# A four-layer graph network on one core: a new written order with layer 1 half a period later, the setup in thirteen steps, and layer 1's head outputs turned by DMA and VectorE

## The chip, the cores and the metric

The kernel runs on one core of a Trainium2 chip. The core has a matrix engine (TensorE, PE in the profile), a vector engine (VectorE, DVE), a scalar engine for activations (ScalarE, ACT), GpSimd (POOL) and a queue engine for transfers (SyncE, SP). Each works through its own instructions in order; semaphores tie them together. The metric is the device time in microseconds from the start of the program to its end; lower is better.

## The reference

Sixty-four graphs of 256 nodes with 256 features pass through four layers. Every layer adds its result to its input and normalizes the rows. `adj` (0 or 1) masks the attention in all of them.

```python
# layer 0: attention with 4 heads of 64, output projection, layer norm
q, k, v = (split(x @ W.T + b) for W, b in ((Wq, bq), (Wk, bk), (Wv, bv)))
attn = softmax(where(adj == 0, -1e9, q @ k.T * 64 ** -0.5))
x = norm(x + layer_norm((attn @ v) @ Wo.T + bo, gamma, beta))
# layer 1: attention with 8 heads of 32 of the normed rows with themselves, then an MLP
n = layer_norm(x, gamma1, beta1)
x2 = x + softmax(where(adj > 0, n @ n.T * 32 ** -0.5, -inf)) @ n      # by head
x = norm(x + x2 + gelu(layer_norm(x2, gamma2, beta2) @ W1 + b1) @ W2 + b2)
# layer 2: additive attention: leaky_relu(s1 + s2), masked softmax, times x @ W
# layer 3: leaky_relu((x * a0) @ x.T) where adj == 1, masked softmax, times x
```

All data are 32-bit floats.

## The kernel before

The 64 graphs make 32 groups of two. A group's work is cut into eleven generators ("threads"), each of which runs one step at a time: `a` (load, mask, layer 0's projections, scores, products of both graphs), and for each graph (0, 1) `u` (layer 0's output projection and norms), `z` (layer 1's input turned), `w` (layer 1's head outputs, norm, its result turned), `o` (the MLP's second product, layers 2 and 3, the store); `b` is layer 1's attention and `c` the MLP's first product with GELU, for both graphs.

What stands after what is written out. `PLACES` gives each step of a group a time in periods, a period being one group; `FIRST` and `LAST` spell the order of the filling and of the emptying pipeline, a letter for a thread and a digit for a group. A wrapper ties each engine's instructions in the order in which the steps issue them, SP's transfers included, so nothing overtakes: an instruction that waits holds up everything behind it on its engine. `BUFS` says how many buffers a tile has; a new tile waits until the oldest one's readers are done.

TensorE wants the contracted axis on partitions, so tiles are turned often. `flipped` does it in one of two ways: by `transpose` on TensorE into PSUM, which ACT copies out, or by `put` (two transfers to DRAM), `get` (four transfers back that place 32x32 blocks) and one block transpose on DVE (`turn_blocks`). The switches `FX`, `FZ`, `FY`, `FN2`, `FN3` choose the second way for x, layer 1's input (z), the MLP's input (xb) and the rows of layers 2 and 3 (xn); `DIRECT` lists exceptions by group. For layer 1's head outputs (oT in `thread_w`), `FO` is False: eight transposes a group on TensorE.

Layer 0's softmax sums go to DRAM and come back to all partitions (`lines`, then `rr`), in `thread_u`, before the head outputs are scaled.

Weights for the first steps are loaded by ACT's queue at the start. All others are gathered in the list `later`, and the generator `prepare` issues them on SP and works out what is derived from them (`bop`, the output bias with the values' bias; W1 times gamma2 and b1; the columns of `wx`; bounds), one of its seven steps after each of the turns in `PREPARE`.

ACT holds one table of functions at a time; between an exponential and a GELU a table load stands in its program.

Of the kernel before, what the change touches and what calls it, by code (L numbers as in the profile page):

```python
# [8 lines left out]
F32 = mybir.dt.float32  # L9
# [4 lines left out]
ALU = mybir.AluOpType  # L14
AX = mybir.AxisListType

P = 128
N = 256
D = 256
NC = D // P  # L20
# [4 lines left out]
W = D + 4  # L25
DFF = 1024
NF = DFF // P
# [12 lines left out]
FO = False  # L40
# [3 lines left out]
DIRECT = {0: ('x', 'z'), 31: ('yT', 'n2', 'n3')}  # L44
BUFS = {'t': 6, 'q': 3, 'k': 2, 'v': 5, 'y': 4, 'z': 4, 'xb': 4, 'both': 2, 'xn': 6, 'mask': 3, 'e': 6, 'x0': 2, 'turned': 1, 'blk': 3, 'oT': 2, 'zs': 2, 'rr': 2, 'xT': 1, 'qT': 1, 'kT': 1}
PLACES = {
    "a": (0.00000, 0.26380, 0.44172, 0.77301, 0.77914, 0.78528, 0.80982, 0.85890, 0.87730, 0.95092, 0.96932,
        0.99386, 1.04295, 1.07362, 1.08589, 1.11043, 1.12883, 1.13497, 1.17178, 1.18405, 1.19018, 1.21472,
        1.25767, 1.27607, 1.28221, 1.29448, 1.31902,),
    "u0": (1.33742, 1.34356, 1.34969, 1.40491, 1.41104, 1.49080, 1.54601, 1.56442, 1.60736, 1.68098,),  # L50
    "u1": (1.36810, 1.41718, 1.51534, 1.55215, 1.57055, 1.60123, 1.63190, 1.65031, 1.67485, 1.79141,),
    "z0": (1.61350, 1.66258, 1.69325, 1.72393,),
    "z1": (1.75460, 1.80368, 1.82209, 1.85276,),
    "b": (1.74847, 1.76074, 1.76687, 1.81595, 1.84049, 1.84663, 1.89571, 1.90184, 1.90797, 1.91411, 1.92024,
        1.92638, 1.93865, 1.95705, 1.96319, 1.98773,),
    "w0": (1.93251, 1.94478, 2.01841, 2.02454, 2.06135, 2.14110, 2.22086, 2.30675,),
    "w1": (2.01227, 2.03068, 2.03681, 2.09203, 2.14724, 2.20245, 2.23313, 2.31288,),
    "c": (2.32515, 2.38037, 2.48466, 2.50920, 2.53374, 2.57669, 2.58896, 2.61963,),
    "o0": (2.63804, 2.65644, 2.69939, 2.73620, 2.82822, 2.86503, 2.88957, 3.04908, 3.19632, 3.20859, 3.30061,
        3.33129, 3.37423, 3.38650, 3.39264, 3.42331, 3.43558, 3.46626, 3.47853, 3.52147, 3.58282, 3.62577,  # L60
        3.64417, 3.66871, 3.71779, 3.98159, 4.05521, 4.07975, 4.09816, 4.10429, 4.11656, 4.12270, 4.25153,
        4.59509,),
    "o1": (2.79755, 2.83436, 2.87117, 2.88344, 2.97546, 3.00614, 3.06749, 3.23926, 3.26994, 3.28834, 3.35583,
        3.36196, 3.42945, 3.44785, 3.45399, 3.46012, 3.47239, 3.49693, 3.50307, 3.55828, 3.68712, 3.70552,
        3.71166, 3.73006, 3.74233, 4.15337, 4.15951, 4.16564, 4.17791, 4.22699, 4.24540, 4.52761, 4.53988,
        5.39877,),
}
PREPARE = (8, 14, 26, 50, 70, 85, 100)
FIRST = (
    "a0a0a0a0a0a0a1a1a1a0a0a0a0a0a0a0a0a1a1a0a0a2a0a0a0a0a0a0a0a0a1a0a0a0U0U0U0a1a1U0a1u0u0a2U0U0u0u0U0U0U0Z0Z0u0"  # L70
    "u0u0u0a2Z0Z0U0b0b0b0b0u0z0b0a2z0z0b0z0b0b0b0b0b0b0W0W0a1b0b0b0a1b0a1W0W0W0W0w0u0w0w0w0W0a1a1a1a1a1a1a1a1a1a1"
    "W0a1w0a1a1a1w0w0w0c0a1c0U1U1c0c0U1U1u1U1U1u1u1c0a2a2c0c0c0u1O0O0U1U1U1Z1a2u1Z1u1U1u1u1O0u1o0O0Z1z1z1Z1b1b1b1"
    "O0z1o0o0o0u1z1b1b1b1a2a2b1b1b1b1b1b1O0O0W1W1b1o0a2b1b1a3a3a2a2b1o0O0a2w1W1W1W1o0o0w1w1w1a2a2a3a2a2a2a2a2W1W1"
    "a2a2w1w1w1O0O0a2a2a2W1o0a4o0U2U2w1a2a2u2u2o0o0c1c1O0O0o0o0o0o0o0c1u2c1o0o0o0U2O0O0O0O0U2c1O0O0O0U2U2c1U2U2O0"
    "O0c1c1u2U2Z2O1o0o0o0O1Z2u2u2O0O0o0a3o1U2O0u2u2o0Z2Z2u2O0O1O1z2a3a3b2b2b2o1o1o1a4z2z2b2b2b2z2a3a3a3b2b2b2b2b2"
    "b2b2b2a4a4O0O0W2O1O1W2O1a3a3b2b2o1o0o0a3a3o1W2W2w2W2W2u2w2w2O1w2O0O0a3a3a3a3o1a3W2W2O0O0w2w2w2a3a3a3a3O1o0o0"
    "o1o0o0O1a3a3a3U3U3o1o1a3w2O1a3c2O1U3o1c2o1O1O1O0O0U3U3U3u3u3u3o0o0o1o1o1o1c2c2O1U3U3c2c2O1O1u3U3Z3o1c2u3u3O1"
    "u3u3c2O1O2O2Z3o1u3Z3Z3O1O1u3b3o1o1O1O2O2z3o1O1O1o2O1O0b3b3b3o1o1z3b3O2z3O2O2o1o1b3o2o2a4z3b3a4b3a4O2b3b3b3b3"
    "b3o2a4a4O1O1b3O1O1a4a4W3b3a4U3W3W3W3o2b3w3o2o2O1a4a4a4a4w3w3a5W3O1w3")
LAST = (  # L80
    "a7w5a6o4o3o3O4O3a6a6a6W5W5o4a6o4o4U6U6w5a6u6u6c5c5o4O4U6o4o4o4O4o2o4o4U6U6U6o4o3c5c5c5O4o3O3c5a7o4o4U6U6U6Z6"
    "u6O4O4O4O4O4u6u6u6o4o4c5u6Z6u6c5O5Z6U6Z6b6O4O4o4O4u6z6z6O5b6b6b6u6O5O5O4z6b6o5b6O5O4O4O4o5a7o4o4a7a7z6b6o5o5"
    "b6a7b6b6b6b6W6W6b6a7a7b6a7a7W6W6O5O5b6b6o4o4o5o5o5a7w6w6w6O5a7a7a7a7O4w6a7a7O4O4O4W6W6a7a7a7w6w6o4O5o4o5O4O5"
    "a7a7O4a7a7W6o5o4o4W6w6w6o5o4a7U7o5U7a7U7o5u7u7c6c6U7O5o4o5O4O4U7O5c6u7c6U7o5o5U7U7U7Z7o5u7u7o3O5u7o5o5Z7O5O5"
    "O5u7u7Z7c6o5c6U7c6O5c6u7z7o5o5O6O6O6O5O6z7z7Z7b7b7o6b7b7u7o5O6O5O5O5b7b7O6O5o6o6o6z7b7O6b7b7O4b7b7W7b7O6W7o6"
    "o6o6b7b7o5o5O5O5O5b7b7w7O6W7O6o6w7o5o6o5o5o5w7W7o6O5W7o5o5w7O5w7o4O5o5W7W7O5O5O5O5w7w7O6w7W7c7c7O6O6o6O6O6o6"
    "c7c7o5O6O6c7O5O5o6o6o6o5o6c7c7c7o6o6O7O6O7O7O6O6o7o6O6O6O6O6O7O7o6o6o7o6O6o7O7O7o6o6O6O6o7o7O6O6O7O7o7O6o6O7"
    "O7O6o7o7O6o7o5o7o7O7o7O7O7O6O6O7O7O7o7o7o6o7o7o7o6o6o6o6o6O7o6O7O7O7o7o7O7o7o7o7O7O7O7o7o7o7O7O7O7o6O7O7o7o7"
    "O7o7O7O7o7o7o7o7O7o7o6o7")
LETTERS = dict(a="a", U="u0", u="u1", Z="z0", z="z1", b="b", W="w0", w="w1", c="c", O="o0", o="o1")  # L90
# [358 lines left out]
def usual_input(ctx: ExitStack, tc: tile.TileContext, a: dict, out: bass.AP, flag: bass.AP):  # L449
# [84 lines left out]
    def load(queue, to, of):  # L534
        if queue:
            queue.dma_start(to, of)
        else:
            later.append((to, of))

    def load_rows(name, cols, queue=None):  # L540

        src = a[name]
        t = const.tile([P, src.shape[0] // P, cols], F32, name=name)
        load(queue, t, src.rearrange("(c p) f -> p c f", p=P))
        return t
# [22 lines left out]
    beta0 = load_all(a["L0_gnn_beta"], "beta0", queue=ACT)  # L568
    woT = load_rows("L0_gnn_WoT", D)
    bv = load_column(a["L0_gnn_bv"], D, "bv")  # L570
    bo = load_all(a["L0_gnn_bo"], "bo", 0)

# [4 lines left out]
    gamma0 = load_all(a["L0_gnn_gamma"], "gamma0")  # L577
    beta1r = load_all(a["L1_gnn_beta1"], "beta1r")
    gamma1r = load_all(a["L1_gnn_gamma1"], "gamma1r", 256)
    b2 = load_all(a["L1_gnn_b2"], "b2", 512)  # L580
    gamma1 = load_column(a["L1_gnn_gamma1"], D, "gamma1")
    beta1 = load_column(a["L1_gnn_beta1"], D, "beta1")
    gamma2 = load_column(a["L1_gnn_gamma2"], D, "gamma2")
    beta2 = load_column(a["L1_gnn_beta2"], D, "beta2")
    b1 = load_column(a["L1_gnn_b1"], DFF, "b1")
    a0 = load_column(a["L3_gnn_a0"], D, "a0")
    w1 = load_rows("L1_gnn_W1", DFF)
    w2 = load_rows("L1_gnn_W2", D)
# [500 lines left out]

    def prepare():  # L1090

        for to, of in later[:3]:
            SP.dma_start(to, of)
        yield
        for to, of in later[3:-2]:
            SP.dma_start(to, of)
        yield
# [8 lines left out]
        for to, of in later[-2:]:  # L1106
            SP.dma_start(to, of)
        wa = setup[:, 1280:2304].rearrange("p (s c d) -> p s c d", s=2, c=NC)
        for s in range(2):
            DVE.tensor_tensor(wa[:, s], wx[:, :, 0:D], a12[:, s:s + 1, :].to_broadcast([P, NC, D]), ALU.mult)  # L1110
        DVE.tensor_reduce(wa1, wa, AX.X, ALU.add)
        for k, (s, share) in enumerate(((0, SLOPE - 1.0), (1, SLOPE), (1, 1.0))):
            DVE.tensor_scalar(wx[:, :, D + k:D + k + 1], wa1[:, s, :].unsqueeze(2), share, None, ALU.mult)

        yield
# [15 lines left out]

        yield
# [23 lines left out]
        yield  # L1156

        pm = new(ps_m, [P, NF], F32, "pm", 4)
        for f in range(NF):
            for c in range(NC):  # L1160
                matmul(pm[:, f:f + 1], w1[:, c, f * P:(f + 1) * P], beta2[:, c:c + 1], start=c == 0, stop=c == NC - 1)
        DVE.tensor_tensor(b1, b1, pm, ALU.add)
        for c in range(NC):
            DVE.tensor_scalar(w1[:, c, :], w1[:, c, :], gamma2[:, c:c + 1], None, ALU.mult)
# [7 lines left out]

    def written(text, since):
        return [(since + int(text[k + 1]), LETTERS[text[k]]) for k in range(0, len(text), 2)]

    preparing = prepare()
    groups = [threads_of(g) for g in range(B // G)]
    plan = [(g, n) for _, g, n in sorted((g + t, g, n) for g in range(B // G) for n, ts in PLACES.items() for t in ts)]
    head, tail = written(FIRST, 0), written(LAST, B // G - 8)
    for turn, (g, name) in enumerate(head + plan[len(head):len(plan) - len(tail)] + tail):  # L1180
        next(groups[g][name], END)
        if turn in PREPARE:
            next(preparing, END)
    assert next(preparing, END) == END
# [54 lines left out]
```

## Time and profile before

| what | us |
|---|---|
| median of 3 runs (2472.14 to 2473.8) | 2473.54 |
| time of the profiled execution | 2474.4 |
| span of the profiled execution, first to last instruction | 2472.5 |
| TensorE busy | 2414.1 (98%) |
| VectorE busy | 2119.0 (86%) |
| ScalarE busy | 1510.2 (61%) |
| GpSimd busy | 747.2 (30%) |

In a page's first part "busy" is time in which at least one instruction of that engine ran; the second part cuts the span into 40 slices, with busy tenths as digits. A row of a group names line, engine, operation, output and input tiles with shapes, how often it came, its busy time, the mean of one in ns, and the idle time ahead of it with what ended it. All recorded operations bear one line number, that of the wrapper, so rows are told apart by tiles. A row of the timeline gives start, length, engine, operation and how many.

### The profile page before, as it was taken

What the parts mean: (1) busy time and instruction counts of PE and PEld (TensorE: products, weight loads), DVE (VectorE), ACT (ScalarE), POOL (GpSimd) and SP (SyncE); (2) the same over time, 40 slices, a digit from 0 to 9 for tenths busy, and PEclk for the clock granted to TensorE, in tenths of its full rate; (3) what the DMA queues carried; (4) which work ended last, traced back from release to release, by engine and by line L of the source; (5) the groups of instructions that cost most, each with busy time, mean ns of one, the idle gap of its engine ahead of it and who ended that gap; (6) DMA issues with size and microseconds to landing.
All of it is one profiled execution on the core that took longest, in us unless ns stands there. A gap on an engine that the chain in (4) does not pass through costs nothing.

```text
span 2472.5 us, 48109 instructions
## 1 busy us (share of the span) xinstructions
PE 2414.1 (98%) x15888; PEld 1811.9 (73%) x15888; DVE 2119.0 (86%) x6238; ACT 1510.2 (61%) x2635; POOL 747.2 (30%) x1804
## 2 busy tenths in 40 slices
PE   5899999999999999999999999999999999999997
PEld 3577777777777777787777777777777777777776
DVE  4788888988888988889988889988888988889884
ACT  3456566666666666666666666665666666666654
POOL 0222233323233233233232333232333232333232
PEclk9899999999999999999999999999999999999999
DMA  6235253444443444443444444444444444434321
GB/s 143 46 82 108 61 112 88 92 98 101 96 103 86 92 97 101 101 103 86 91 96 102 103 96 91 89 99 103 103 87 96 92 99 101 106 85 92 81 65 44
DMA packets 903791, 229.78 MB, mean 93 GB/s; under 512 B 707313, under 2 KB 903153, under 8 KB 903537
## 3 DMA queue, kind: packets, MB, share of 16 engines
q1 hardware_dynamic: 902032, 225.73, 41.8%
q8 instruction: 128, 2.10, 0.4%
q14 instruction: 127, 1.03, 0.1%
q10 hardware_dynamic: 1504, 0.92, 0.1%
HBM read 136.07 MB, written 82.05 MB: 88 GB/s over the span
## 4 chain that ended last, share of the span: by engine, by line
PE 72%; ACT 8%; DVE 6%; DMA 5%; SPq 4%; POOL 3%; issue 2%; ACTq 0%; DVEq 0%; POOLq 0%
PE pm L473 65%; PE ps L473 7%; SPq L473 4%; DMA blk<-rows 3%; ACT e L473 2%; ACT adj L473 1%; DVE y L473 1%; DVE e L473 1%; ACT adjb L473 1%; POOL rstd L473 1%; ACT xn L473 1%; DVE st L473 1%; ACT xb L473 1%; POOL nm L473 1%; ACT oT L473 1%
## 5 line engine op out<-in xcount | busy, mean ns | idle before, releaser
L473 POOL TENSOR_SCALAR ve<-mv 128x2 f32<-128x2 f32 x448 | 149.3, 333 | 1613.9 <-DVE mv L473 1104.9
L473 PE MATMUL pm<-L_gnn_W,hT 128*128 128x256 f32 x2048 | 468.0, 382 | 0.0
L473 PE MATMUL pm<-t,L_gnn_W 128*128 128x256 f32 x2048 | 458.2, 379 | 1.6 <-DVE t L473 1.6
L473 ACT ACTIVATE e<-ps 128x1024 f32<-128x1024 f32 x384 | 373.0, 1021 | 126.1 <-PE ps L473 125.4
L473 PEld LDWEIGHTS pm<-L_gnn_W,hT 128*128 128x128 f32 x2048 | 382.0, 190 | 67.0 <-issue 18.9
L473 PEld LDWEIGHTS pm<-t,L_gnn_W 128*128 128x128 f32 x2048 | 386.5, 190 | 53.9 <-DVE t L473 2.1
L473 DVE SCALAR_TENSOR_TENSOR e<-e,mask 128x256 f32<-128x256 f32 x1024 | 364.7, 420 | 12.7 <-ACT e L473 12.4
L473 POOL TENSOR_TENSOR rstd<-ve,mhalf 128x2 f32<-128x2 f32 (+1 forms) x384 | 344.9, 898 | 32.0
L473 ACT ACTIVATE xn<-y,nm,rstd 128x256 f32<-128x256 f32 x256 | 139.5, 593 | 278.0 <-POOL xn L473 223.0
L473 DVE BATCH_NORM_STATS2 st<-y 128x6 f32<-128x256 f32 x640 | 236.3, 411 | 4.7
L473 DVE STREAM_TRANSPOSE t<-blk 128x512 f32<-128x512 f32 x248 | 172.1, 703 | 75.1 <-DMA blk<-rows 74.9
L473 ACT ACTIVATE hT<-pm,b 128x512 f32<-128x512 f32 x256 | 163.9, 676 | 28.5 <-PE pm L473 25.1
L473 PE MATMUL ps<-t 32*128 32x256 f32 x2048 | 156.8, 406 | 5.2 <-ACT t L473 4.0
L473 DVE TENSOR_TENSOR e<-e,mask 128x1024 f32<-128x1024 f32 x128 | 149.7, 1213 | 0.5 <-ACT e L473 0.5
L473 PEld LDWEIGHTS ps<-t 32*128 32x128 f32 x2048 | 100.7, 187 | 61.1 <-ACT qT L473 18.9
L473 DVE SCALAR_TENSOR_TENSOR y<-pm,r,xn 128x256 f32<-128x256 f32 x256 | 123.8, 484 | 9.4
L473 PE MATMUL pm<-wx,t 128*128 128x259 f32 x512 | 127.7, 392 | 2.4
L473 PE MATMUL ps<-qT,kT 64*128 64x256 f32 x1024 | 129.4, 393 | 0.5 <-ACT e L473 0.5
L473 PE MATMUL pm<-e,v 128*32 128x256 f32 x2048 | 125.9, 386 | 2.2
L473 PE MATMUL pm<-e,z 128*32 128x256 f32 x2048 | 127.5, 385 | 0.1
L473 PE MATMUL pm<-xn,q 128*128 128x257 f32 x512 | 127.0, 380 | 0.0
L473 ACT COPY v<-pm 128x259 f32<-128x259 f32 (+1 forms) x192 | 81.3, 442 | 71.9 <-PE pm L473 71.9
(133 smaller groups left out, 4207.5 us busy)
## 6 DMA issues: line engine op xcount, KB each, us to landing
blk<-rows SPq DMA_DIRECT2D x992, 64.0 KB
rows<-xn SPq DMA_DIRECT2D x248, 128.0 KB
x<-in_x SPq DMA_DIRECT2D x32, 512.0 KB
adj<-in_adj SPq DMA_DIRECT2D x32, 512.0 KB
rr<-lines SPq DMA_DIRECT2D x128, 128.0 KB
out<-xn SPq DMA_DIRECT2D x64, 256.0 KB
turned<-in_x SPq DMA_DIRECT2D x248, 64.0 KB
rows<-xb SPq DMA_DIRECT2D x124, 128.0 KB
```

What stands on the lines that cost most here:

```text
L473: ins = call(*args, **kw)
```

## The change

The switch `FO` is set: in groups 1 to 30 `thread_w` writes the head outputs to DRAM, reads them back in blocks and turns them on DVE; groups 0 and 31 ('o' in `DIRECT`) keep the TensorE way. All places and both spelled orders are new. In them layer 1 (`z`, `b`, `w`) stands about half a period further from layer 0 and `c` and `o` follow, so that a group's last step comes at 6.3 periods in place of 5.4. The list of loads is cut into eight parts (W1 and W2 in halves) and the derived values into five; both become threads `l` and `p` of group 0 with places of their own in `FIRST`. One buffer moves from t to the masks.

```diff
-FO = False
+FO = True
-DIRECT = {0: ('x', 'z'), 31: ('yT', 'n2', 'n3')}
-BUFS = {'t': 6, ... 'mask': 3, ...}
+DIRECT = {0: ('x', 'z', 'o'), 31: ('yT', 'n2', 'n3', 'o')}
+BUFS = {'t': 5, ... 'mask': 4, ...}
 PLACES = {
...
-    "z0": (1.61350, 1.66258, 1.69325, 1.72393,),
+    "z0": (2.46061, 2.66667, 2.69091, 2.89091,),
...
-    "w0": (1.93251, 1.94478, 2.01841, 2.02454, 2.06135, 2.14110, 2.22086, 2.30675,),
+    "w0": (3.46667, 3.50909, 3.58788, 3.61212, 3.63030, 3.71515, 3.77576, 3.86667, 3.89697,),
...
-    "c": (2.32515, 2.38037, 2.48466, 2.50920, 2.53374, 2.57669, 2.58896, 2.61963,),
+    "c": (4.03030, 4.03636, 4.06061, 4.07273, 4.19394, 4.20000, 4.20606, 4.25455,),
...
-PREPARE = (8, 14, 26, 50, 70, 85, 100)
 FIRST = (
-    "a0a0a0a0a0a0a1a1a1a0a0a0a0a0a0a0a0a1a1a0a0a2a0a0a0a0a0a0a0a0a1a0a0a0U0U0U0a1a1U0a1u0u0a2U0U0u0u0U0U0U0Z0Z0u0"
+    "a0a0l0a0a0a0a0a0a0a1a0a0a0l0a1a0l0a0a0a0a1a0a0a0a0a0a0a0a0a1a1a0U0U0a0a1a0a0u0u0a2a1a1l0a1p0U0U0a2a2u0u0a3a1"
...
+    def load_rows(name, cols, queue=None, parts=1):
...
+        for k in range(parts):
+            if k:
+                later.append([])
+            some = slice(k * n // parts, (k + 1) * n // parts)
+            load(queue, t[:, some], of[:, some])
         return t
...
+    def loading():
+        for some in later:
+            for to, of in some:
+                SP.dma_start(to, of)
+            yield
+
     def prepare():
-
-        for to, of in later[:3]:
-            SP.dma_start(to, of)
-        yield
-        for to, of in later[3:-2]:
-            SP.dma_start(to, of)
-        yield
...
-    preparing = prepare()
     groups = [threads_of(g) for g in range(B // G)]
+    groups[0].update(l=loading(), p=prepare())
...
-    for turn, (g, name) in enumerate(head + plan[len(head):len(plan) - len(tail)] + tail):
+    since = sum(n not in "lp" for _, n in head)
+    for g, name in head + plan[since:len(plan) - len(tail)] + tail:
         next(groups[g][name], END)
-        if turn in PREPARE:
-            next(preparing, END)
```

The body of `prepare` keeps its arithmetic; the part for W1 and b1 moves from last place to second.

## The prediction

> **What bounds the kernel now.** I read the page's first two parts, then busy times by stretch, then one steady period, then the first 50 us of SP's queue.
>
> ```profile
> span 2472.5 us, 48109 instructions
> ...
> PE 2414.1 (98%) x15888; PEld 1811.9 (73%) x15888; DVE 2119.0 (86%) x6238; ACT 1510.2 (61%) x2635; POOL 747.2 (30%) x1804
> ...
> PE   5899999999999999999999999999999999999997
> ```
>
> ```profile
> 0.00:112.00 112.00, 76.81 (x499) 45.09 (x500) 64.86 (x173) 45.02 (x71) 15.12 (x34) 0.86 0.45 99
> 112.00:2350.00 2238.00, 2231.30 (x14802) 1681.19 (x14803) 1974.38 (x5791) 1400.48 (x2442) 697.05 (x1657) 1.00 0.43 95
> 2350.00:2472.50 122.50, 106.01 (x590) 85.65 (x588) 79.76 (x277) 64.72 (x123) 34.99 (x114) 0.97 0.23 55
> ```
>
> The columns are the stretch, its length, the busy time of PE, PE's weight loads, DVE, ACT and POOL, then granted clock, DMA share and GB/s. From 112 to 2350 us TensorE is idle for 6.7 us in all; of its 58 idle us the head holds 35.2 and the tail 16.5. A steady group costs what its matmuls stream; the ends cost their gaps. In the head the clock falls too:
>
> ```profile
> 60.00:70.00 10.00, 4.25 (x26) 2.37 (x28) 8.71 (x28) 4.71 (x7) 5.37 (x12) 0.64 1.01 156
> 70.00:80.00 10.00, 7.92 (x62) 4.44 (x64) 6.81 (x38) 6.91 (x10) 0.23 (x2) 0.50 0.01 2
> ```
>
> Busy time by missing clock, over the slow 10 us stretches of the head (0.66 at 30 us, 0.83 at 40, 0.64 at 60, 0.50 at 70, 0.85 at 90), is 10.5 us. The head's loss is 35.2 + 10.5 = 46 us.
>
> One period, from one group's first query matmul to the next group's:
>
> ```profile
> 1187.77:1262.27 74.50, 74.33 (x495) 56.20 (x494) 66.11 (x195) 46.94 (x82) 23.63 (x56) 1.00 0.45 96
> ```
>
> PE is full; DVE has 8.4 us to spare, ACT 27.6.
>
> **The change, part by part.**
>
> *Head outputs off TensorE.* Groups 1 to 30 lose eight transposes each; groups 0 and 31 keep theirs. The groups by shape, and the timeline around two blocks of four:
>
> ```profile
> L473 PE MATMUL pm<-ident,oT 128*128 128x128 f32 x256 | 40.6, 280 | 0.9 <-ACT oT L473 0.8
> L473 DVE STREAM_TRANSPOSE t<-blk 128x512 f32<-128x512 f32 x248 | 172.1, 703 | 75.1 <-DMA blk<-rows 74.9
> L473 ACT ACT_TABLE_LOAD x65 | 83.4, 1283 | 7.2 <-issue 4.5 <-PE pm L473 1.7
> ```
>
> ```profile
> 1270.04 0.66 PE L473 MATMUL pm<-ident,oT 128*128 128x128 f32 x4
> 1270.53 3.60 PE L473 MATMUL pm<-xT,L_gnn_WkT 128*128 128x512 f32 x8
> ...
> 1277.82 0.60 PE L473 MATMUL pm<-ident,oT 128*128 128x128 f32 x4
> 1278.25 1.89 PE L473 MATMUL pm<-L_gnn_WvT,xT 128*128 128x256 f32 x8
> ```
>
> Durations of piped matmuls overlap, so I take start to next start: 0.49 + 0.43 = 0.92 us a period. Thirty periods: -27.6 us, on the path wherever PE is full. The period goes from 74.50 to 73.58.
>
> In their place each half group gets two writes to DRAM, four reads and one block transpose. DVE: 703 ns long, 0.63 from start to start (1262.79 to 1263.42), twice a period: +1.3 us, so 67.4 of 73.6. Of its waits in the period from 1262 to 1337, PE accounts for 4.1 us, which shrink by themselves; others (POOL's rstd 1.2, blocks 1.1, xn 0.7, e 0.2) for 3.2. 67.4 + 3.2 = 70.6 is under 73.6: hidden, with 3.0 us left. Were DVE the bound, the 1.3 would cost 40 us over thirty periods. The multiplication by 1/sum now reads SBUF in place of PSUM: 692 against 688 ns in the rows y<-y,xb and y<-pm,r, nothing.
>
> SP: six issues at medians of 0.40 and 0.49 us, 2.8 us for a half group and 5.5 a period, into a queue that stood waiting for 34 us of such a period: hidden. The writes wait for ACT's scaled head outputs; queued behind them on SP are the next writes of z and xn and their reads, and for those DVE's block transposes, behind which stand the mask products that PE needs. Write, landing (2.1 us) and reads (1.9 + 2.3) take 7 us; the places of the new order give 0.042 + 0.079 periods, 9 us, so nothing is late. Block reads rise from 32 to 40 a period; were all of the DMA share 0.45 theirs, it would be 0.56.
>
> The skill's page "VectorE: DVE Perf Modes" (The three transpose paths) speaks against this: it sends a full transpose to TensorE and calls a plain copy with transposing strides 19 times slower than the transposing DMA. Here the strides only place 32x32 blocks, DVE turns them, and the row shows 2.2 us landings that DVE waits for 74.9 us in 248. By the rule I would book a late block each time (say 1 us each for sixty, +60); by the row nothing. I follow the row.
>
> *Layer 1 half a period on, deeper pipeline.* The same PE instructions in another order; stages from attention to MLP stand further apart, 6.3 periods from load to store in place of 5.4. What it costs is on ACT: in the built order the score exponentials now fall between the pairs of GELUs, and table loads go from 2 to 4 a group: +60 of 1.283 us, 2.6 us a period of ACT's 27.6 spare. Locally it is tight. Between two of layer 1's score blocks ACT has, one behind the other, two exponentials (2.05), a load (1.28), two GELUs (1.35), three pairs of scalings (3.55), two GELUs, a load: 10.9 us. From the first block's end PE has an output projection (1.73), sixteen MLP matmuls (6.9), a projection and the next block (1.08): 11.4 us. ACT starts about 1 us late (a load stands before it too), so the exponentials come some 0.6 us late and, after the head products (1.88) that hide most, the block after next waits 0.35 us at worst for its score buffer. Between 0 and 0.35 over thirty periods is 0 to 10 us; the row nearest (a 1.36 us score block at 1268.74, where others take 1.15) shows 0.2 us of the same wait already paid, so I take 5. What is late next is the score buffer, then layer 1's products.
>
> The page "ScalarE: Activation LUTs" (What ACT_TABLE_LOAD costs) puts a switch at 1.28 us and a 1.38 us drain. In the trace each load begins 0.02 us after the instruction ahead of it and the next starts 0.01 us behind it when its input is there: 1.28 it is. By the page two more switches add 2.8 us to that stretch, PE would wait some 3 us a period, +90 us, and the change would lose. I use the row.
>
> Buffers: t goes from 6 to 5 while flips rise from 8 to 10 a group, masks from 3 to 4. A late t costs the wait for its reader on PE, at most a score or MLP block (1.1 to 3.5 us), at best nothing; PE reads each t soon after it is made, so nothing is booked beyond the 5 above.
>
> *The setup in thirteen steps.* No instruction is saved but the loads move. SP's head (start, length, issues):
>
> ```profile
> 20.31 5.04 SPq L473 DMA_TRANSPOSE adjT<-adjb  x4
> ...
> 35.47 1.33 SPq L473 DMA_DIRECT2D a<-in_L_gnn_a  x1
> 36.84 4.77 SPq L473 DMA_DIRECT2D turned<-in_x  x8
> 41.66 0.49 SPq L473 DMA_DIRECT2D x<-in_x  x1
> 42.25 0.45 SPq L473 DMA_DIRECT2D adj<-in_adj  x1
> 42.80 0.65 SPq L473 DMA_DIRECT2D lines<-zs  x1
> 47.56 1.30 SPq L473 DMA_DIRECT2D rr<-lines  x2
> ```
>
> Fifteen setup loads hold SP from 25.40 to 36.80, and group 0's sums leave at 42.80. In the new order three and then five loads (the first half of W1 among them) go out while SP waits for the mask (to 9.71, to 20.31); the rest stands behind group 0's sums. Then DVE's reciprocal (39.36 now, about 33 when the matmul for the output bias no longer stands ahead) sets it: group 0 gains some 7 us here. It gives part of it back, since DVE now does group 1's masks and exponentials between: my walk has its first MLP matmul (109.13 now) at 109 to 115. But by that matmul PE has done more: group 1's two output projections (3.5), group 2's Q, K, V (3 x 3.5), scores (4.0), products and sums (4.7), one score block (1.1), 23.8 us that now come behind it. So the head saves between 23.8 - 6 = 18 and 24; later steps of a filling pipeline may give some back, so I take 17, bounds 0 and 25.
>
> *Tail.* The written order ends like the present one (layers 2 and 3 of the last group, its flips on PE in both): 16.5 us of idle stay, -3 to +5, taken as 0.
>
> **Sum.** On the profiled execution: 2474.4 (1.9 around the span), and the median shown is 0.9 lower. 2473.5 - 27.6 - 17 + 5 = 2434.
>
> **The rivals.**
> - *The head gives nothing* (the chain of group 0, not PE's filling, sets when the steady part begins): 2473.5 - 27.6 + 5 = 2451. For it: DVE is at 8.71 of 10 at 60 us. Against it: PE is half idle there with group 1's input at hand.
> - *The period stays 74.5*, since a wait of 0.92 us takes the transposes' place: 2473.5 - 17 = 2456. For it: the tight ACT stretch, DVE's 3.0 us. Against: PE's total waits of 1.6 us from 150 to 2350.
> - *Head at its best*, no new waits, tail -3: 2473.5 - 27.6 - 25 - 3 = 2418.
> - *Slower*: ACT is in order, and the scalings between the GELU pairs wait for POOL's statistics (up to 6.6 us now, at 1233.69, where nothing hung on it). Now a GELU, a load and the exponentials hang on it, and PE's score buffers on these. It decides at (27.6 + 17 + 5) / 30 = 1.65 us of PE wait a period; at 2 us: 2473.5 - 44.6 + 60 = 2489.
>
> **How the numbers follow.** Forecast 0.52, head nothing 0.18, period stays 0.12, best head 0.12, slower 0.06 (0.02 of it within 0.2%, about what measurement can tell). Faster: 0.52 + 0.18 + 0.12 + 0.12 = 0.94; same 0.02; slower 0.04. The range takes in the best head and the stuck period with some room on either side, 2410 to 2462, and leaves out about 0.14.
>
> **What would show it.** Right: a period of 73.6 to 73.8 us with PE full, first-112-us PE idle under 25 with a clock above 0.86, 125 table loads of 1.28 us, 308 block transposes. Wrong: gaps on PE behind e or ps in the MLP stretch (the slower rival), DVE waits for blocks well over 1.1 us a period, a first MLP matmul later than 118 us, or a tail with over 22 us idle.

## The result and the profile after

The changed kernel takes 2440.73 us (median, 2438.21 to 2443.91) against 2473.47 us before: a ratio of 0.9869 with a 95% interval of 0.9852 to 0.9886, 32.7 us less. A second set of runs gave 2441.04 us and 0.9864 (0.9849 to 0.9879). The forecast was 2434, in a range of 2410 to 2462. Its total was 7 us too low: one of its four terms, the new waits on TensorE, was a third of its true size, and by luck a head that came out better than forecast hid part of that. The terms can be read from the profile.

The first two parts of the page after:

```profile
span 2439.0 us, 47947 instructions
...
PE 2380.2 (98%) x15648; PEld 1784.9 (73%) x15648; DVE 2151.0 (88%) x6298; ACT 1575.9 (65%) x2695; POOL 722.7 (30%) x1804
...
PE   7999999999999999999999999999999999999997
```

240 matmuls are gone (15888 to 15648, eight in each of thirty groups). TensorE is busy for 33.9 us less and the span is 33.5 us shorter. Its idle time, span less busy, is 58.8 us where it was 58.4: as much as before, in other places. The stretches of the profile show where. Head, middle and tail, and between them one period, have the columns of the same view before (PE, its weight loads, DVE, ACT, POOL, clock, DMA share, GB/s):

```profile
0.00:112.00 112.00, 91.77 (x656) 55.75 (x660) 81.47 (x189) 57.14 (x94) 16.23 (x40) 0.96 0.47 121
112.00:2320.00 2208.00, 2187.60 (x14453) 1645.57 (x14446) 2001.60 (x5879) 1456.97 (x2484) 676.22 (x1659) 1.00 0.50 110
2320.00:2439.00 119.00, 100.87 (x545) 83.53 (x543) 67.94 (x231) 61.82 (x117) 30.28 (x105) 0.95 0.18 46
1257.20:1331.05 73.85, 73.39 (x488) 55.19 (x486) 67.17 (x197) 49.14 (x84) 22.94 (x56) 1.00 0.50 111
```

- The head's idle time is 112 - 91.77 = 20.2 us, from 35.2.
- The middle's is 20.4 us, from 6.7.
- The tail's is 18.1 us, from 16.5.
- The period went from 74.50 to 73.85 and TensorE's part of it from 74.33 to 73.39. Before, TensorE missed 0.17 us of a period; now it misses 0.46.

TensorE's waits between 112 and 2320 us say what the middle's new idle time is (in total, times, longest):

```profile
PE pm L475 <- ACT oT L475: 11.7, 25, 0.5
PE pm L475 <- ACT v L475: 5.4, 1, 5.4
```

One is a gap of 0.47 us that comes once a period, 25 times. The other is one gap of 5.4 us. Together they are 17.1 us of the 20.4.

### The profile page after: what moved, and what is told of

Same layout as the page of the kernel before. It is cut to its first block, busy times and chain, and to the rows that moved or that the text cites. A ratio compares the mean times of both kernels' runs of the same rounds, so it can differ in the third digit from the quotient of the medians.

```text
span 2439.0 us, 47947 instructions
## 1 busy us (share of the span) xinstructions
PE 2380.2 (98%) x15648; PEld 1784.9 (73%) x15648; DVE 2151.0 (88%) x6298; ACT 1575.9 (65%) x2695; POOL 722.7 (30%) x1804
## 4 chain that ended last, share of the span: by engine, by line
PE 80%; ACT 6%; DVE 5%; DMA 4%; issue 2%; SPq 2%; POOL 1%; DVEq 0%; POOLq 0%; ACTq 0%
PE pm L475 71%; PE ps L475 9%; ACT e L475 2%; SPq L475 2%; DMA rows<-xb 2%; DVE e L475 1%; ACT t L475 1%; DVE y L475 1%; ACT xn L475 1%; DMA blk<-rows 1%; DVE st L475 1%; DVE t L475 1%; POOL nm L475 1%; POOL rstd L475 1%; ACT oT L475 1%
## 5 line engine op out<-in xcount | busy, mean ns | idle before, releaser
L475 POOL TENSOR_SCALAR ve<-mv 128x2 f32<-128x2 f32 x448 | 130.6, 292 | 1604.2 <-DVE mv L475 1305.5
L475 PE MATMUL pm<-L_gnn_W,hT 128*128 128x256 f32 x2048 | 455.8, 381 | 0.0
L475 POOL TENSOR_TENSOR rstd<-ve,mhalf 128x2 f32<-128x2 f32 (+1 forms) x384 | 316.3, 824 | 32.0
L475 DVE STREAM_TRANSPOSE t<-blk 128x512 f32<-128x512 f32 x308 | 216.2, 703 | 22.3 <-DMA blk<-rows 22.2
L475 ACT ACTIVATE qT<-pm,bq 128x512 f32<-128x512 f32 x64 | 43.5, 687 | 201.7 <-PE pm L475 201.7
L475 ACT ACT_TABLE_LOAD x125 | 160.4, 1283 | 8.7 <-DMA L_gnn_WqT<-in_L_gnn_WqT 5.9
L475 POOL TENSOR_SCALAR nm<-nm 128x2 f32<-128x2 f32 x320 | 140.0, 438 | 28.0
L475 PE MATMUL pm<-wx,t 128*128 128x259 f32 x512 | 128.5, 394 | 13.1 <-ACT oT L475 11.7
L475 PE MATMUL pm<-xn,q 128*128 128x257 f32 x512 | 132.7, 384 | 5.4 <-ACT v L475 5.4
```

The costliest lines, as they stand in the source:

```text
L475: ins = call(*args, **kw)
```

## The experiments

**The changed kernel once more**, as the base of the three versions after it.

> The changed kernel itself, once more, so that the three runs beside it have a base on the same chip. 2438 to 2443 us, a period of 73.85 us, TensorE idle 0.46 us a period ahead of the first pm<-wx,t and 5.4 us once near 2165 us.

It gave 2441.04 us (2439.78 to 2443.22), as expected.

**The gap of every period.** The timeline of the changed kernel around one of these gaps, TensorE and ACT only (start, length, engine, operation, how many; in brackets the idle time before it and what ended it):

```profile
1277.25 1.93 PE L475 MATMUL pm<-e,v 128*32 128x256 f32 x32
1277.89 1.09 ACT L475 ACTIVATE xn<-y,nm,rstd 128x256 f32<-128x256 f32 x2 [0.50 <-DMA rows<-xb]
1278.89 1.08 ACT L475 ACTIVATE t<-t,beta,gamma 128x256 f32<-128x256 f32 x2
...
1279.87 0.56 ACT L475 COPY oT<-pm 128x512 f32<-128x512 f32 x1
1280.48 2.02 PE L475 MATMUL pm<-wx,t 128*128 128x259 f32 x8 [0.47 <-ACT oT L475]
```

The matmuls with `wx` write a `pm` buffer in PSUM. The oldest of these holds layer 0's products from 1277.25, and ACT frees it by copying them out to `oT`. That copy starts at 1279.87, since ACT first does two scalings and the pair with beta and gamma that stands after them, 2.0 us. That pair is the last step of `z0`; the first matmul that reads its result starts at 1282.43, 2.5 us after the pair ends. The test moves this one step ahead on ACT, between the two pairs of exponentials of layer 0's scores:

```diff
-    "z0": (2.46061, 2.66667, 2.69091, 2.89091,),
+    "z0": (2.46061, 2.66667, 2.69091, 2.80000,),
```

> The scaling of layer 1's first turned input (z0's last step) is moved in the steady order from just ahead of ACT's copy of layer 0's head outputs to a gap after the first pair of score exponentials. Theory: TensorE's wait of 0.46 us a period is for a PSUM buffer that this copy frees, and the copy is late only because the two scalings (1.08 us) stand ahead of it on ACT; the period goes from 73.85 to 73.39 and the time down by 25 x 0.47 = 12 us. Rival: the copy is late because of the products or the xn ahead of it, or the wait moves to the next instruction; then within 2 us of the base.

It gave 2424.62 us (2423.88 to 2427.54), ratio 0.9805 (0.9792 to 0.9819), 16.4 us less than the changed kernel beside it. One period of this kernel, then the same place in its timeline:

```profile
1250.51:1323.77 73.26, 73.26 (x487) 55.18 (x486) 67.14 (x197) 49.23 (x84) 22.93 (x56) 1.00 0.51 112
```

```profile
1270.57 1.93 PE L475 MATMUL pm<-e,v 128*32 128x256 f32 x32
1271.20 1.10 ACT L475 ACTIVATE xn<-y,nm,rstd 128x256 f32<-128x256 f32 x2 [0.50 <-DMA rows<-xb]
...
1272.57 0.59 ACT L475 COPY oT<-pm 128x512 f32<-128x512 f32 x1 [0.28 <-PE pm L475]
...
1273.21 2.02 PE L475 MATMUL pm<-wx,t 128*128 128x259 f32 x8
```

The copy now starts 2.0 us after the products instead of 2.6, and it waits for TensorE where TensorE waited for it. The gap is gone and TensorE is full, 73.26 of 73.26. So the cause is shown: a buffer that was held because one ACT step stood in the wrong place. Of the gain 11.7 us are these gaps, as expected. The other 4.7 us lie in TensorE's busy time (2375.1 in place of 2380.2, several kinds of matmul shorter by 2 to 4 ns each), and what shortened them isn't shown.

**The one gap of 5.4 us.** VectorE around it in the changed kernel, and how the stall reaches ACT and TensorE:

```profile
2155.23 0.19 DVE L1201 TENSOR_REDUCE tops<-edges 128x1 f32<-128x32 f32 x1 [8.29 <-ACT adj L475]
...
2163.24 1.09 ACT L475 ACTIVATE xb<-y,nm,rstd 128x256 f32<-128x256 f32 x2 [7.57 <-POOL nm L475]
...
2164.94 1.62 PE L475 MATMUL pm<-xn,q 128*128 128x257 f32 x3 [5.41 <-ACT v L475]
```

Line 1201 is not the wrapper's. It belongs to the end of the program, where some running sums and maxima are reduced to one flag. These instructions were issued without the wrapper, so the written order does not bind them, and one of them stood early in VectorE's program. It needs the last group's edge sums, which ACT makes in a pass over `adj` and had not made yet, so VectorE stood still for 8.29 us; POOL's statistics came late, then ACT's scaling, and TensorE lost 5.41 us. The kernel before has the same lines (its line 1192); there the instruction ran at 2261.5 us and waited for nothing. The test issues them through the wrapper, which puts them behind all other work:

```diff
-    nc.vector.tensor_reduce(tops[:, 3:4], edges, AX.X, ALU.max)
+    DVE.tensor_reduce(tops[:, 3:4], edges, AX.X, ALU.max)
...  (and so for the other reductions and comparisons of that block)
```

> The final checks' reductions on VectorE are tied into the written order, so that they run after all groups and not where they fall. Theory: the one over the edge sums stands in VectorE's program at 2155 us and holds it 8.3 us for the last group's mask on ACT, which makes the 5.4 us gap of TensorE at 2165; without it 5 to 6 us less, the steady period unchanged. Rival: the gap is caught up in the idle tail anyway and the reductions now lengthen the end: within 1 us of the base, or 1 us more.

It gave 2436.18 us (2434.03 to 2438.16), 4.9 us less. The period with the stall went from 81.3 to 73.18 us: of these 8.1 us 5.4 are the gap, and most of the rest is a lower clock just behind it (the last section has its rows). The end paid 0.8 us more for the reductions that now stand there (the last wait went from 4.7 to 5.5). Where the other 2.4 us of the 8.1 went isn't shown.

**Both together.**

> Both edits. If both theories hold they add: 12 + 5 = 17 us less than the base, near 2423 us. If only one holds, its own share.

It gave 2419.39 us (2417.9 to 2421.45), ratio 0.9781 (0.9767 to 0.9794): 21.7 us less than the changed kernel where the two alone gave 16.4 + 4.9 = 21.3. It is the fastest version here. Its stretch from 112 to 2320 us:

```profile
112.00:2320.00 2208.00, 2203.92 (x14624) 1662.87 (x14617) 2015.48 (x5931) 1474.10 (x2508) 683.96 (x1681) 1.00 0.50 110
```

TensorE is idle there for 4.1 us in all.

**The new order with the head outputs on TensorE.** Everything as changed, except that every group takes the old way for them.

```diff
-DIRECT = {0: ('x', 'z', 'o'), 31: ('yT', 'n2', 'n3', 'o')}
+DIRECT = {g: ('o',) for g in range(32)}
+DIRECT[0], DIRECT[31] = ('x', 'z', 'o'), ('yT', 'n2', 'n3', 'o')
```

> The changed kernel with the head outputs of all groups turned on TensorE again, everything else (order, setup, buffers) as changed. Theory: the transposes cost TensorE 0.92 to 0.94 us a period and nothing hides them, so the period is 74.8 (73.39 + 0.94 + the 0.46 wait) and the time 28 us above the changed kernel, about 2469; the head's gain stays. Rival: the new flips cost what they save (DVE, SP), then within 8 us of the changed kernel.

It gave 2480.3 us (2476.01 to 2482.24), ratio 1.0024 (1.0015 to 1.0032): slower than before, and 39 us above the changed kernel where 28 were expected. One period of it, then where its second gap lies:

```profile
1281.26:1356.53 75.27, 74.44 (x496) 56.06 (x494) 65.73 (x194) 49.13 (x84) 22.05 (x56) 1.00 0.43 95
```

```profile
1346.18 0.55 PE L476 MATMUL pm<-ident,oT 128*128 128x128 f32 x3 [0.36 <-ACT oT L476]
1346.56 2.78 PE L476 MATMUL pm<-t 128*128 128x256 f32 x16
1349.18 0.60 PE L476 MATMUL pm<-ident,oT 128*128 128x128 f32 x4
```

The period has both gaps, 0.47 and 0.36, and TensorE streams 74.44. In this order the move off TensorE is worth 75.27 - 73.85 = 1.42 us a period: 74.44 - 73.39 = 1.05 of streaming, and 0.36 that the transposes wait for the head outputs. Thirty times that is 43 us; 39 were measured, and the gap of 5.4 us is missing here: the instruction behind it held VectorE for 2.2 us in place of 8.3, and TensorE did not stand for it. So the new order alone loses: its period is 0.77 us longer than before, 23 us over thirty, more than its better head returns.

**The move in the old order.** The kernel before with `FO` set, writes and reads in one step, since the old places have no step between them; order and setup as before.

```diff
-FO = False
+FO = True
-DIRECT = {0: ('x', 'z'), 31: ('yT', 'n2', 'n3')}
+DIRECT = {0: ('x', 'z', 'o'), 31: ('yT', 'n2', 'n3', 'o')}
...
                 SP.dma_start(rows[:, c].rearrange("q p j -> p q j"), oT[:, c, :].rearrange("p (q j) -> p q j", q=QB))
-            yield
             blk = get(rows)
```

> The kernel before with the flip of the head outputs through DRAM and VectorE alone: old order, old setup; write and read of the blocks are issued in one step, since the old order has one step less. There the turned tile is wanted 0.9 us after the write is issued, and takes about 7. Theory: VectorE stands some 5 us for each half group, 10 a period, of which its 8 spare us hide most, and TensorE waits 2 to 5 us a period: slower than before by 40 to 130 us. So the shift of layer 1 is what makes the flip pay. Rival: VectorE runs enough ahead that the wait is hidden, then 28 us faster than before.

It gave 2789.78 us, ratio 1.1281 (1.1262 to 1.13): 316 us slower, far over the 40 to 130 expected. VectorE's, TensorE's and SP's largest waits over the run, then one of them in the timeline:

```profile
DVE t L473 <- DMA blk<-rows: 331.3, 123, 12.2
...
PE pm L473 <- DVE e L473: 91.6, 28, 5.5
...
SPq L473 <- ACT oT L473: 295.6, 81, 8.8
...
SPq L473 <- DMA rows<-oT: 98.5, 60, 3.5
```

```profile
1505.29 0.89 SPq L473 DMA_DIRECT2D rows<-oT  x2
1509.46 2.05 SPq L473 DMA_DIRECT2D blk<-rows  x4
...
1513.38 0.71 DVE L473 STREAM_TRANSPOSE t<-blk 128x512 f32<-128x512 f32 x1 [4.89 <-DMA blk<-rows]
...
1515.94 2.60 PE L473 MATMUL pm<-e,z 128*32 128x256 f32 x12 [4.80 <-DVE e L473]
```

From the first write to the block transpose are 8.1 us, where the forecast had 7 to the end of the reads, and the work that is written ahead of it on VectorE ends at 1508.5. VectorE stands for 4.89 us, the mask products behind it are late, and TensorE stands for 4.80. SP stands too, since each read is written right behind its write: 98.5 us in 60 waits.

**The same with room.** Three versions give the old order what it seemed to lack: the reads get a step 3.5 us after the writes, the block transpose comes 9 us after them, and every later step of the group moves by 0.05, 0.10 or 0.15 periods (t 5 and mask 4, as in the changed kernel).

```diff
+for _n, _own in (("w0", (1.93251, 1.98000, 2.05500)), ("w1", (2.01227, 2.06000, 2.13500))):
+    PLACES[_n] = _own + tuple(round(t + 0.1, 5) for t in PLACES[_n][2:])
+for _n in ("c", "o0", "o1"):
+    PLACES[_n] = tuple(round(t + 0.1, 5) for t in PLACES[_n])
...  (and the filling and the emptying order get the one more step of w0 and w1)
```

> The head outputs' flip in the old order, as before, but with its reads a step of their own (3.5 us after the writes) and its block transposes 9 us after them, and with all later steps of the group 0.10 periods later; buffers as after (t 5, mask 4), setup as before. Theory (the flip in the old place was 316 us slower because its blocks were asked for too soon): the waits for blocks fall from 10.8 us a period to under 3 and the period from 85 to 74 to 76, total 2460 to 2530. Rival (the old order of the engines has no place for the flip at all, wherever its reads stand): the period stays above 79 and the total above 2600.

> The same with the later steps 0.15 periods later, since a shift also mixes the later stages differently with the next groups' early ones. Theory: within 30 us of the shift by 0.10, and under 2530. Rival: above 2600.

> The same with the later steps 0.05 periods later: 3.7 us less than the reads and the block transpose take. Theory: some of the waits for blocks come back where the norm and the MLP's input now follow too closely, 2480 to 2580, above the shift by 0.10. Rival: above 2600.

One run of each gave 3097.36 us (0.10), 3086.85 (0.15) and 3002.76 (0.05): all three over 400 us above the theory's 2460 to 2580, and over 200 above the version without room. The theory failed, and the rival's number was met without its reason being shown. With 0.10, the waits for blocks did fall, to 215.7 us over the run (from 331.3), but others took their place. VectorE's largest waits in it:

```profile
DVE e L477 <- ACT e L477: 415.7, 124, 6.9
DVE t L477 <- DMA blk<-rows: 215.7, 72, 10.9
```

VectorE's mask products wait for exponentials. Why these are late isn't shown: moving the late stages by a fixed amount also moves their ACT steps past those of the early stages, but no version took that apart. So it stays open whether the old order could have taken the move with better places. What is shown is that in this program, where nothing overtakes, the places of a few steps count for hundreds of us, where the transposes taken off TensorE are worth 39.

**The setup's loads.** As changed, but the five parts of the list that come behind group 0's sums go out with the third part, ahead of them.

```diff
-        for some in later:
+        for some in (later[0], later[1], sum(later[2:], [])):
...
+        for _ in later[3:]:
+            yield
```

> The changed kernel with the third to eighth part of the setup loads issued in one lump at the third's place, ahead of group 1's transposes, as the kernel before had it. Theory: ten more issues of 0.5 us stand ahead of group 0's sums on SP, which leave at about 38 to 40 us in place of 34.07, and 1.5 MB more compete with the second group's input; the first MLP matmul comes 4 to 7 us later than 113.34, the time 4 to 7 us more. Rival: TensorE has group 1's work to do meanwhile and the head does not depend on it: within 2 us.

It gave 2446.27 us (2445.35 to 2448.09), ratio 0.9887 (0.9871 to 0.9904): 5.5 us more than the changed kernel. In the changed kernel group 0's sums leave and MLP matmuls begin at

```profile
34.07 0.65 SPq L475 DMA_DIRECT2D lines<-zs  x1
...
113.34 3.72 PE L475 MATMUL pm<-t,L_gnn_W 128*128 128x256 f32 x16
```

and with the loads in one lump at

```profile
37.05 0.65 SPq L475 DMA_DIRECT2D lines<-zs  x1
...
121.07 3.72 PE L475 MATMUL pm<-t,L_gnn_W 128*128 128x256 f32 x16
```

Three us more on SP become 7.7 at the first MLP matmul and 5.5 at the end (4 to 7 were expected of both).

**Two more table loads.** As changed, with one GELU on one column, which nothing reads, behind the exponentials of the third score block. It makes ACT load a table and load the old one again, 64 more loads in all (189 in place of 125).

```diff
                     es.append(exp_of(pss[k], 32 ** -0.5, mask[:, i, :], s["sums", i], c, k))
+                    if (i, c, k) == (1, 0, 1):
+                        ACT.activation(spare, ones[:, 0:1], AF.Gelu)
```

> The changed kernel with one more GELU over a single column after the exponentials of layer 1's third score block, in every group, so two more table loads (66 more pairs of 1.28 us in ACT's program; the column is not used). It measures the margin of ACT in that stretch. Theory: each load is 1.28 us and no more, ACT's busy time rises by 2.7 us a period, the last exponentials end about 2.8 us later and VectorE's masks behind them pass the moment at which TensorE wants them (1319.55) by 0.5 to 1.5 us: 15 to 45 us more. Rival (ACT has 24 us to spare in a period, so loads are free): within 5 us. Rival (a load costs 2.66 us with its drain): over 60 us more.

It gave 2491.21 us (2489.89 to 2493.55), ratio 1.0071 (1.0054 to 1.0088): 50 us more, over the 15 to 45 expected. Its timeline, ACT at the added instruction, then TensorE at what it delays; and one period:

```profile
1336.79 1.28 ACT L475 ACT_TABLE_LOAD   x1
1338.08 0.20 ACT L475 ACTIVATE spare<-ones 128x1 f32<-128x1 f32 x1
1338.19 0.82 ACT L475 ACTIVATE oT<-pm,gamma 128x256 f32<-128x256 f32 x2
1339.03 1.28 ACT L475 ACT_TABLE_LOAD   x1
1340.33 1.02 ACT L475 ACTIVATE e<-ps 128x1024 f32<-128x1024 f32 x1
...
1344.99 2.77 PE L475 MATMUL pm<-e,z 128*32 128x256 f32 x32
...
1348.22 1.13 PE L475 MATMUL pm<-t 128*128 128x256 f32 x4 [0.46 <-ACT t L475]
```

```profile
1282.63:1357.86 75.23, 74.23 (x488) 55.37 (x487) 67.27 (x197) 51.70 (x87) 24.09 (x56) 1.00 0.50 110
```

A load takes 1.28 us and the next activation starts 0.01 to 0.02 us after it; nothing more is paid. The rival's 2.66 us, the load and the drain of "ScalarE: Activation LUTs" (What ACT_TABLE_LOAD costs) that the prediction names, isn't seen. ACT's busy time grows by 51.70 - 49.14 = 2.56 = 2 x 1.28, and the period by 1.38: the head products stretch from 1.93 to 2.77 us and a gap of 0.46 follows. So about 1.2 of the 2.56 us fit in at this place, though ACT is idle for 24.7 us of a period of the changed kernel. Thirty periods of 1.38 make 41 of the 50 us; where the rest lies isn't shown.

## Why the prediction was right, and where its sum was off

Term by term, with what the runs showed ("slow clock" is busy time by missing clock):

| step of the forecast | forecast | measured |
|---|---|---|
| head outputs off TensorE | -27.6 | -28.2: 74.33 - 73.39 = 0.94 a period, thirty times |
| head (setup, order) | -17 (0 to -25) | -21.6: idle time 35.2 to 20.2, slow clock 10.5 to 3.9 |
| new waits on TensorE | +5 (0 to 10) | +16.8: middle idle 6.7 to 20.4, slow clock 0 to 3.1 |
| tail | 0 (-3 to +5) | +3: idle 16.5 to 18.1, slow clock 1.4 to 2.8 |
| sum | -39.6 | -30.0 (span: -33.5; the other 3.5 are in no term) |

- *Transposes: right.* The cost of what took their place is where the forecast put it: VectorE at 67.17 us of a period (67.4 was said), and its waits for blocks smaller, not larger. The block transposes and the table loads over the run:

```profile
L475 DVE STREAM_TRANSPOSE t<-blk 128x512 f32<-128x512 f32 x308 | 216.2, 703 | 22.3 <-DMA blk<-rows 22.2
...
L475 ACT ACT_TABLE_LOAD x125 | 160.4, 1283 | 8.7 <-DMA L_gnn_WqT<-in_L_gnn_WqT 5.9
```

  Sixty more transposes, and all of them wait for 22.2 us where it was 74.9. So the rule on transposes that would have booked +60 does not hold in the new order. In the old order, where little work stands between write and use, the blocks were late (331.3 us in 123 waits) and the cost was worse than +60. The factor of 19 that the forecast quotes from "VectorE: DVE Perf Modes" (The three transpose paths) is stated there for copies whose innermost destination stride is large. The block reads here write 32 neighbouring values at a time, and no run here has such a copy.
- *Table loads: right.* 125 loads at 1283 ns. That a load costs 1.28 and not 1.28 plus a drain is measured twice, in this row and by the two added loads. But the cover that the forecast named for them, "27.6 us spare", was much too wide a view. Its local count of 10.9 against 11.4 us was the useful one, and the added loads show how little room there was.
- *The head: right in kind, 4 to 5 us better.* Group 0's sums left SP at 34.07 us, 8.7 earlier than before where some 7 were said, and the first MLP matmul came at 113.34, within 109 to 115. The working gave 18 to 24; the 17 that was taken allowed for a loss that did not come. The loads in one lump show that 5.5 us of it hang on SP's order. The rest, the new order of the filling steps, was not tested apart.
- *The step that failed: "I take 5" for new waits.* The forecast looked for them behind the score buffers in the MLP stretch. There the wait stayed at 0.2 us (one score block of 1.36 us where others take 1.15). The wait came at another shared buffer, `pm`, with another culprit on the same engine: not the GELUs and their loads but the last scaling of `z0`, which the new places put ahead of a copy that frees PSUM. It was 11.7 us, over the bound of 10. With that one step moved, the period is 73.26, under the forecast's 73.58.
- *A term that was missing: 5.4 us*, and 3.1 of slow clock behind them, from instructions at the program's end that the diff does not touch. That instructions issued outside the wrapper may stand anywhere in VectorE's program could be read in the code; the forecast put them at nothing.
- *Not tested apart:* the buffer that moved from t to the masks. In the middle TensorE waits for VectorE's `t` once, for 0.9 us.

Of the rivals, "the head gives nothing" and "the period stays 74.5" are ruled out by the stretches. The slower one, TensorE waiting for ACT's order by over 1.65 us a period, did not come: TensorE misses 0.46. Two table loads more add 1.38 us a period and make the kernel slower than before, so it was near.

## What to carry to other kernels

When a program ties every engine's order, do not cost a reordering by engine totals. For each engine in order, ask which instruction frees a shared buffer, and what now stands ahead of it. PSUM copies that free a buffer belong ahead of scalings that nobody waits for yet. Taking work off the bounding engine needs places for what replaces it: here the move in the old places and the new order without the move each lose, and together they win.

Bind everything, the last few reductions included. One instruction left outside the order held VectorE for 8.3 us in the middle of the run.

## What was not expected of the hardware

One gap can cost more than its length, since TensorE's granted clock can fall behind it. Around the gap of 5.4 us the changed kernel reads

```profile
2160.00:2165.00 5.00, 0.06 (x1) 0.09 (x1) 4.93 (x15) 1.76 (x4) 3.36 (x7) 0.95 0.44 85
2165.00:2170.00 5.00, 5.00 (x18) 3.62 (x20) 4.93 (x9) 2.74 (x4) 1.00 (x2) 0.50 0.47 92
2170.00:2175.00 5.00, 5.00 (x40) 3.24 (x40) 4.93 (x12) 4.28 (x10) 3.26 (x8) 0.87 0.19 52
```

TensorE is busy for all of the 10 us after the gap, the first 5 at a clock of 0.50 and the next at 0.87. Busy time by missing clock, 2.5 + 0.65, is 3.1 us beside the 5.4 of the gap. The version with the final reductions in order has no such gap, and there the same three stretches read 1.00. So this fall comes with the gap. The gaps of 0.47 us once a period never lowered the clock: between 120 and 2160 us every stretch of 5 us reads 1.00. (Over the whole middle the dip at 2165 us is averaged away, so the row of the middle reads 1.00 too.)

In the head the link is less plain:

```profile
70.00:80.00 10.00, 10.00 (x53) 7.05 (x52) 8.52 (x26) 3.31 (x6) 1.03 (x2) 0.83 0.46 151
...
100.00:110.00 10.00, 6.33 (x68) 2.79 (x72) 9.87 (x12) 3.58 (x8) 0.00 (x0) 0.81 0.57 102
110.00:112.00 2.00, 2.00 (x24) 0.94 (x20) 0.75 (x2) 0.00 (x0) 0.00 (x0) 0.50 0.02 5
```

At 110 us TensorE is busy all the time at a clock of 0.50, after 3.7 us of idle time in the ten before. But from 28 to 42 us it was idle for 4.0 us of 14, and the clock stayed at 1.00 up to 70 us. What lowers it in the head stays open.
